# Row transforms of a spectral layer as pairs of 64-column products, and the last loads moved to ScalarE's queue

## The chip, the cores and the metric

One core of a Trainium2 chip runs the whole program. The metric is device time in microseconds (us) of one execution. Everything is computed in 32-bit floats (F32), except for some operands of the attention that the kernel splits in two parts.

## What is computed

The input is an image of 48 x 48 tokens (T = 2304) with C = 768 channels. A transformer block comes first: layer norm, attention over all tokens with relative positions, a projection, and an MLP with a hidden width of 3072. A spectral layer follows, and the change lies at its two ends. Cut to what matters:

```python
# layer 0
x = shortcut + attention(layernorm(x)) @ proj_w + proj_b
x = x + gelu(layernorm(x) @ mlp_w1 + mlp_b1) @ mlp_w2 + mlp_b2
# layer 1 (H = W = 48, 8 blocks of 96 channels)
bias = x
xf = rfft2(x, axes=(1, 2), norm='ortho').reshape(B, 48, 25, 8, 96)
o1r = relu(xr @ w1[0] - xi @ w1[1] + b1[0]);  o1i = relu(xi @ w1[0] + xr @ w1[1] + b1[1])
o2r = softshrink(o1r @ w2[0] - o1i @ w2[1] + b2[0], 0.01);  o2i = ...
y = irfft2(o2r + 1j * o2i, s=(48, 48), axes=(1, 2), norm='ortho')
return y + bias
```

## The kernel before, in words

**Stages.** The program runs in one order: queries, keys and values, attention, projection, the MLP, the spectral layer. The block's result stays on chip as `x1` (128 tokens x 18 tiles x 768 channels, in the tile `main`). The channels of the spectral layer are worked in two halves of CH = 384.

**The order of the work.** TensorE's order in the MLP and in the spectral layer is written out by hand (`tc.manual_schedule(engines={PE})`, lines 1109 and 1306). The other engines and the queues are ordered by the framework's scheduler, which may bring a load forward in SyncE's queue. In the whole kernel every transfer is issued on SyncE's queue (named SP, or SPq where its issues are listed). Each engine works through its own queue in order, and an issue of a transfer waits for its data, for its buffer, and for an earlier transfer whose semaphore it uses again; there are eight such semaphores, used in turn.

**Forward row transform** (`rows_forward`, line 1069). The MLP runs in three blocks p of 768 tokens, and after each one the rows of that block are transformed along the width. A row has 48 tokens, and its 25 frequencies have a real and an imaginary part: 50 numbers. A group g of 384 tokens is 8 rows, three tiles of 128 tokens. The result of a group is cut into four parts `zp` of two rows (100 partitions x 384 channels), each of which takes one or two products with a constant of 128 x 100, `rows_dft[:, b]`: six products per group and channel half. Each part is copied out of its PSUM bank (tags o0 to o3, one bank each, which the MLP's second layer shares) into a tile `zt` (eight buffers), by ScalarE for p = 0 and 1 and by VectorE and ScalarE in turn for p = 2, and stored to `z1` in HBM, where a row takes 50 lines of 384 channels.

**Middle of the spectral layer** (class `Unit`, line 1180). Fourteen units (two channel halves, seven sets of up to four frequencies; the last set has one) pass through four steps. `load` fetches `zi` from z1 (`load_frequencies`, line 937; the first two units' loads are issued within `rows_forward` at p = 2). `columns` transforms along the height (`fp`), `first` and `second` are the two layers (`lp`, `l1`, `mp`), and `back` transforms back along the height (`yp`, one PSUM bank) and stores `y` to `z2` in HBM. In round r of the main loop unit r is at `columns`, r - 1 at `first`, r - 2 at `second` and r - 3 at `back`, with four steps i in a round.

**Inverse row transform** (`rows_back`, line 1281). For a group of 384 tokens and one channel half, one load brings `zo` (100 partitions x 4 x 384) from z2, which needs that all frequencies of that half are in z2. Then three output tiles `rps` of 128 tokens take two products each (100 x 128 constants `irows`), VectorE adds x1 into `yt` (four buffers), and SyncE stores it to the output. `rps` has the two banks of tag f, which `fp` also uses, and zo has three buffers. The generators of the first half are advanced by one step in each step i of the rounds r > 11: one step in four is a load, three are pieces (a piece is one output tile). So 12 pieces stand in TensorE's order ahead of the last `yp`, and 24 after it: six of the first half and 18 of the second.

Of the kernel before, what the change touches and what calls it, by code (L numbers as in the profile page):

```python
# [9 lines left out]
F32 = mybir.dt.float32  # L10
# [34 lines left out]
def block_then_afno(  # L45
# [47 lines left out]

    z1 = [dram.tile([HW * 2 * KW, CH], F32, name=f"z1_{k}") for k in range(2)]
    z2 = [dram.tile([HW * 2 * KW, CH], F32, name=f"z2_{k}") for k in range(2)]
# [841 lines left out]
    def load_frequencies(half, k0):  # L937

        rows = z1[half].rearrange("(r k) c -> r k c", k=KW)
        tiles = []  # L940
        for k in range(k0, min(k0 + 4, KW), 2):
            n = min(2, KW - k)
            zi = turn.tile([P, C], F32, name="zi", tag="turn")
            zi = zi[: 2 * HW].rearrange("p (k c) -> p k c", c=CH)
            nc.sync.dma_start(out=zi[:, :n], in_=rows[:, k : k + n, :])
            tiles.append(zi)
        return tiles

    with ExitStack() as mlp:
        bias = mlp.enter_context(tc.tile_pool(name="mlp_const", bufs=1))  # L950
        b2 = bias.tile([P, C], F32, name="b2")
        nc.sync.dma_start(out=b2, in_=mlp_b2[0, :].partition_broadcast(P))
        rows_dft = bias.tile([P, 6, 2 * 2 * KW], F32, name="rows_dft")
        nc.sync.dma_start(out=rows_dft, in_=c_rows)
# [114 lines left out]
        def rows_forward(p):  # L1069

            for k in range(2):
                for g in (2 * p, 2 * p + 1):
                    for a, parts in enumerate(((0,), (1, 2), (3, 4), (5,))):
                        zp = psum.tile([2 * 2 * KW, CH], F32, name="zp", tag=f"o{a}")
                        for b in parts:
                            nc.tensor.matmul(  # L1076
                                zp, rows_dft[:, b, :], x1[:, 3 * g + b // 2, ts(k, CH)],
                                start=(b == parts[0]), stop=(b == parts[-1]),
                            )
                        zt = turn.tile([2 * 2 * KW, CH], F32, name="zt", bufs=8)  # L1080
                        if p < 2:
                            nc.scalar.copy(zt, zp)
                        else:
                            balanced_copy(a, zt, zp)
                        nc.sync.dma_start(out=z1[k][ts(4 * g + a, 4 * KW), :], in_=zt)
                if (p, k) == (2, 0):
                    first_loads.extend(load_frequencies(0, k0) for k0 in (0, 4))
# [39 lines left out]
    with ExitStack() as sp:  # L1127
# [153 lines left out]
        def rows_back(half, g):  # L1281

            zo = zin.tile([4 * KW, 4, CH], F32, name="zo", bufs=3)
            nc.sync.dma_start(
                out=zo, in_=z2[half][ts(g, 16 * KW), :].rearrange("(a p) c -> p a c", a=4)
            )
            yield
            for i in range(3):
                yt = mid.tile([P, CH], F32, name="yt", bufs=4)
                rp = psum.tile([P, CH], F32, name="rps", tag="f")  # L1290
                for e in range(2):
                    nc.tensor.matmul(  # L1292
                        rp, irows[:, 2 * i + e, :], zo[:, i + e, :], start=(e == 0), stop=(e == 1)
                    )
                nc.vector.tensor_tensor(yt, rp, x1[:, 3 * g + i, ts(half, CH)], ALU.add)
                nc.sync.dma_start(out=out[ts(3 * g + i, P), ts(half, CH)], in_=yt)
                yield
# [3 lines left out]

        def pieces(gens):
            for gen in gens:
                yield from gen

        with tc.manual_schedule(engines={mybir.EngineType.PE}):
            first_half = pieces(ends[0])
            for r in range(len(units) + 3):
                if r < len(units):
                    units[r].load()  # L1310
                for i in range(4):
                    for stage, lag in (("back", 3), ("second", 2), ("first", 1), ("columns", 0)):
                        if 0 <= r - lag < len(units):
                            getattr(units[r - lag], stage)(i)
                    if r > len(units) // 2 + 4:
                        next(first_half, None)
            for _ in first_half:
                pass
            for _ in pieces(ends[1]):
                pass  # L1320


def _constants():
# [18 lines left out]

    fr = np.stack([cos[:, :KW], -sin[:, :KW]], 1).reshape(n, 2 * KW)

# [5 lines left out]

    fwd = np.zeros((8 * n, 8 * 2 * KW))
    inv = np.zeros((8 * 2 * KW, 8 * n))
    for r in range(8):
        fwd[r * n : (r + 1) * n, r * 2 * KW : (r + 1) * 2 * KW] = fr
        inv[r * 2 * KW : (r + 1) * 2 * KW, r * n : (r + 1) * n] = ir
    rows = np.zeros((P, 6, 4 * KW))
    irows = np.zeros((4 * KW, 6, P))
    for b in range(6):
        t, a = b // 2, (b + 1) // 2
        rows[:, b] = fwd[t * P : (t + 1) * P, a * 4 * KW : (a + 1) * 4 * KW]  # L1360
        irows[:, b] = inv[a * 4 * KW : (a + 1) * 4 * KW, t * P : (t + 1) * P]
# [87 lines left out]
```

## Time and profile before

| | us |
|---|---|
| median of three runs | 2929.87 |
| the three runs | 2922.76, 2929.87, 2933.12 |
| the profiled execution | 2924.9 |
| its span, first to last instruction | 2922.9 |
| zp stage at p = 0, first zp product to first product behind the stage | 1965.66 to 1981.47 |
| zp stage at p = 1 | 2313.21 to 2328.69 |
| zp stage at p = 2 | 2655.91 to 2671.5 |
| middle of the spectral layer, first fp to end of the last yp | 2672.1 to 2881.15 |
| tail: end of the last yp to end of span | 2881.15 to 2922.9 |

All times of places are counted from the span's start. A product in F32 leaves two records in the trace, each with its own load of weights, so a stage of 24 products shows 48. The ends of records on TensorE are modelled and overlap the next one's start, so durations are best read from start to start. "Idle before" names what ended an engine's wait.

### The profile page before, as it was taken

Reading aid. Unit: us, or ns where it says so; the run is one execution under the profiler, and the core shown is the slowest. Engines: PE = TensorE matmul, PEld = TensorE weight load, DVE = VectorE, ACT = ScalarE, POOL = GpSimd, SP = SyncE. Lnnn points to the kernel's source line nnn. Section 1 sums busy time; section 2 is a strip of 40 time slices with the busy share of each in tenths; the row PEclk is TensorE's granted clock in tenths of the full one; section 3 lists DMA queues with packets and bytes.
Section 4 is the critical chain, followed back from the end, with each engine's and each line's share of the span. In section 5 each row is a group of like instructions: output and inputs, shape, how many; then the busy total and the mean of one; then the engine's idle time right before and its main releaser. Section 6 shows DMA issues by size and latency. Waiting matters only on the chain. (4 is left out here: it accounts for less than half of the span.)

```text
span 2922.9 us, 40961 instructions
## 1 busy us (share of the span) xinstructions
PE 2864.6 (98%) x15659; PEld 1724.2 (59%) x15659; DVE 1791.0 (61%) x2606; ACT 936.3 (32%) x1514; POOL 609.8 (21%) x564
## 2 busy tenths in 40 slices
PE   7999999999999999999999999999999999999998
PEld 4555665555555555555555555555555555556885
DVE  5243237777777777777733666674666566665564
ACT  1011126656666565665500211122011211102331
POOL 2302110000000000000043322343332323222441
PEclk9999999999999999999999999999999999999999
DMA  3423276173462716435252111212121212113235
GB/s 127 148 88 118 92 162 123 30 135 64 82 128 41 144 34 101 109 59 87 56 177 76 43 56 53 65 64 65 57 65 54 77 54 65 54 57 99 79 93 179
DMA packets 202818, 253.03 MB, mean 87 GB/s; under 512 B 21618, under 2 KB 180978, under 8 KB 201078
## 3 DMA queue, kind: packets, MB, share of 16 engines
q1 hardware_dynamic: 202614, 250.32, 33.5%
q8 instruction: 126, 2.06, 0.3%
q14 instruction: 78, 0.64, 0.1%
HBM read 136.40 MB, written 50.14 MB: 64 GB/s over the span
## 5 line engine op out<-in xcount | busy, mean ns | idle before, releaser
L635 DVE TENSOR_TENSOR acc<-acc,main 128x768 f32<-128x768 f32 x576 | 551.9, 958 | 206.4 <-ACT main L569 149.9
L569 ACT ACTIVATE main<-sp 128x768 f32<-128x768 f32 x648 | 520.8, 812 | 138.9 <-PE sp L565 132.2
L565 PE MATMUL sp<-terms,select 64*128 64x384 f32 x1296 | 413.3, 630 | 0.0
L1051 DVE TENSOR_TENSOR main<-o,main 128x384 f32<-128x384 f32 x540 | 299.4, 557 | 40.3 <-PE o L1049 2.1
L989 PE MATMUL h<-shared,w 128*128 128x384 f32 x864 | 296.7, 486 | 0.8 <-issue 0.8
L559 PE MATMUL sp<-shared 64*128 64x384 f32 x1296 | 268.0, 490 | 2.5 <-DVE o L457 2.2
L559 PE MATMUL sp<-qT,kT 64*128 64x384 f32 x1296 | 266.7, 487 | 0.2
L612 POOL TENSOR_TENSOR inverse<-inverse,rden 128x384 f32<-128x384 f32 x36 | 46.3, 1287 | 1010.7 <-DVE rden L609 918.1
L446 PE MATMUL m<-main 128*128 128x384 f32 x756 | 247.0, 488 | 6.4 <-DVE rstd L121 3.0
L989 PEld LDWEIGHTS h<-shared,w 128*128 128x128 f32 x864 | 164.4, 190 | 116.1 <-issue 2.3
L989 PE MATMUL h<-shared,w1s 128*128 128x384 f32 x648 | 226.6, 486 | 0.0
L582 PE MATMUL op<-main,shared 128*64 128x384 f32 x1296 | 221.2, 488 | 0.0
L582 PE MATMUL op<-main,v 128*64 128x384 f32 x1296 | 219.9, 488 | 0.0
L995 ACT ACTIVATE hT<-c,vec 128x384 f32<-128x384 f32 x108 | 66.4, 615 | 466.2 <-DVE c L1001 466.1
L446 PEld LDWEIGHTS m<-main 128*128 128x128 f32 x756 | 142.6, 190 | 108.3 <-issue 8.7
L1001 DVE TENSOR_TENSOR c<-h,u 128x384 f32<-128x384 f32 x108 | 60.2, 557 | 212.3 <-PE h L989 212.3
L1049 PE MATMUL o<-w,hT 128*128 128x384 f32 x432 | 175.0, 487 | 3.0 <-DVE mv L118 2.0
L1049 PE MATMUL o<-w2s,hs 128*128 128x384 f32 x432 | 174.8, 487 | 3.1 <-DVE hs L155 3.1
L565 PEld LDWEIGHTS sp<-terms,select 64*128 64x128 f32 x1296 | 125.8, 187 | 83.9 <-issue 0.5
L989 PEld LDWEIGHTS h<-shared,w1s 128*128 128x128 f32 x648 | 123.1, 190 | 85.9
L154 POOL TENSOR_TENSOR w1s<-w 128x384 f32<-128x384 f32 x36 | 36.4, 1010 | 610.9 <-PE o L1049 289.4
L559 PEld LDWEIGHTS sp<-shared 64*128 64x128 f32 x1296 | 117.9, 187 | 61.3 <-issue 23.1
(158 smaller groups left out, 3896.8 us busy)
## 6 DMA issues: line engine op xcount, KB each, us to landing
w<-in_mlp_w_dram SPq DMA_DIRECT2D x72, 768.0 KB
terms<-col_parts SPq DMA_DIRECT2D x432, 72.0 KB
terms<-row_hi SPq DMA_DIRECT2D x216, 72.0 KB
terms<-row_lo SPq DMA_DIRECT2D x216, 72.0 KB
main<-in_qkv_w_dram SPq DMA_DIRECT2D x36, 384.0 KB
z<-zt SPq DMA_DIRECT2D x48, 150.0 KB
zo<-z SPq DMA_DIRECT2D x12, 600.0 KB
x<-in_x_dram SPq DMA_DIRECT2D x18, 384.0 KB
```

Of the source, the lines that this page charges most:

```text
L446: nc.tensor.matmul(bank, a[:, c, :], b[:, c, :], start=(first and c == 0), stop=(c == 2), skip_group_check=not first,)
L559: nc.tensor.matmul(sp[:, j, :G], kT[at, ts(kt, P)], qT[at, ts(c, G)], start=True, stop=False,)
L565: nc.tensor.matmul(sp[:, j, :G], select[at, a % 2], ready[pr, c][at, a // 2, b], start=False, stop=True,)
L569: nc.scalar.activation(p, sp[:, :, :G], AF.Exp, scale=HD**-0.5)
L582: nc.tensor.matmul(op[ts(j, 64)], v[:, kt0 + i, ts(j, 64)], ps[i][:, j, :], start=(kt0 + i == 0), stop=(kt0 + i == NT - 1),)
L612: nc.gpsimd.tensor_tensor(inverse, inverse, rden, ALU.add)
L635: nc.vector.tensor_tensor(acc, made[0] if kt == 1 else acc, p, ALU.add)
L989: nc.tensor.matmul(bank[i], a[:, c, :], b[:, c, :], start=(start and c == 0), stop=(c == 2), skip_group_check=not start,)
L995: nc.scalar.activation(h[:, i, ts(k, G)], src, AF.Gelu, bias=col(V_B1 + 2 * n + i))
L1001: nc.vector.tensor_tensor(t, src, other, ALU.add)
L1049: nc.tensor.matmul(bank[k], a, b, start=start, stop=True, skip_group_check=not start)
L1051: nc.vector.tensor_tensor(dst, bank[k], dst, ALU.add)
```

## The change

It has four parts.

1. Forward rows: the result of one row, padded from 50 to 64 lines, is one product with a constant of 128 x 64 (`rows_dft[:, i, r]`: tile i of three, row r of eight). Each output bank holds two rows, one in each half of the 128 partitions, and so in each half of TensorE's columns. Ten products per group replace six; they stand in TensorE's order as five pairs whose two products write different halves. z1 now has 64 lines a row. zt becomes one tile of four parts with two buffers.
2. Inverse rows: an output tile's two halves of 64 tokens are products of their own with 100 x 64 constants. Eight products per group, as four pairs of different halves, replace six. The three output tiles use the tags f, m and l, two banks each.
3. Buffers and queues: two of every five zo tiles take a buffer of zt's, so that there are five; the loads of the second channel half are issued on ScalarE's queue instead of SyncE's.
4. Order: three loads of the first half are started together in round 12, and three pieces a round are done in rounds 13 to 16, in their steps 0 to 2. Four loads of the second half are started ahead of what is left of the first half. In the changed kernel's instruction order nine pieces stand ahead of the last yp, and 27 after it.

```diff
@@ -91,7 +91,7 @@
 
     dram = ctx.enter_context(tc.tile_pool(name="scratch", bufs=1, space=DRAM))
 
-    z1 = [dram.tile([HW * 2 * KW, CH], F32, name=f"z1_{k}") for k in range(2)]
+    z1 = [dram.tile([HW * 64, CH], F32, name=f"z1_{k}") for k in range(2)]
     z2 = [dram.tile([HW * 2 * KW, CH], F32, name=f"z2_{k}") for k in range(2)]
     q_d = [dram.tile([P, T], F32, name=f"q_d{i}") for i in range(NC)]
     k_d = [dram.tile([P, T], F32, name=f"k_d{i}") for i in range(NC)]
@@ -936,7 +936,7 @@
 
     def load_frequencies(half, k0):
 
-        rows = z1[half].rearrange("(r k) c -> r k c", k=KW)
+        rows = z1[half].rearrange("(r k) c -> r k c", k=32)
         tiles = []
         for k in range(k0, min(k0 + 4, KW), 2):
             n = min(2, KW - k)
@@ -950,7 +950,7 @@
         bias = mlp.enter_context(tc.tile_pool(name="mlp_const", bufs=1))
         b2 = bias.tile([P, C], F32, name="b2")
         nc.sync.dma_start(out=b2, in_=mlp_b2[0, :].partition_broadcast(P))
-        rows_dft = bias.tile([P, 6, 2 * 2 * KW], F32, name="rows_dft")
+        rows_dft = bias.tile([P, 3, 8, 64], F32, name="rows_dft")
         nc.sync.dma_start(out=rows_dft, in_=c_rows)
 
         psum = mlp.enter_context(tc.tile_pool(name="ps_mlp", bufs=1, space=PSUM))
@@ -1070,19 +1070,28 @@
 
             for k in range(2):
                 for g in (2 * p, 2 * p + 1):
-                    for a, parts in enumerate(((0,), (1, 2), (3, 4), (5,))):
-                        zp = psum.tile([2 * 2 * KW, CH], F32, name="zp", tag=f"o{a}")
-                        for b in parts:
+
+
+                    zp = []
+                    for pair in (((0, 0), (0, 1)), ((0, 2), (1, 3)), ((1, 2), (1, 5)),
+                                 ((1, 4), (2, 5)), ((2, 6), (2, 7))):
+                        for i, r in pair:
+                            if r // 2 == len(zp):
+                                zp.append(psum.tile([P, CH], F32, name="zp", tag=f"o{len(zp)}"))
                             nc.tensor.matmul(
-                                zp, rows_dft[:, b, :], x1[:, 3 * g + b // 2, ts(k, CH)],
-                                start=(b == parts[0]), stop=(b == parts[-1]),
+                                zp[r // 2][ts(r % 2, 64)], rows_dft[:, i, r],
+                                x1[:, 3 * g + i, ts(k, CH)],
+                                start=((i, r) not in ((1, 2), (2, 5))),
+                                stop=((i, r) not in ((0, 2), (1, 5))), skip_group_check=True,
                             )
-                        zt = turn.tile([2 * 2 * KW, CH], F32, name="zt", bufs=8)
+                    zt4 = turn.tile([P, 4, CH], F32, name="zt", bufs=2)
+                    for a in range(4):
+                        zt = zt4[:, a]
                         if p < 2:
-                            nc.scalar.copy(zt, zp)
+                            nc.scalar.copy(zt, zp[a])
                         else:
-                            balanced_copy(a, zt, zp)
-                        nc.sync.dma_start(out=z1[k][ts(4 * g + a, 4 * KW), :], in_=zt)
+                            balanced_copy(a, zt, zp[a])
+                        nc.sync.dma_start(out=z1[k][ts(4 * g + a, P), :], in_=zt)
                 if (p, k) == (2, 0):
                     first_loads.extend(load_frequencies(0, k0) for k0 in (0, 4))
 
@@ -1280,31 +1289,54 @@
 
         def rows_back(half, g):
 
-            zo = zin.tile([4 * KW, 4, CH], F32, name="zo", bufs=3)
-            nc.sync.dma_start(
+            if (T // G * half + g) % 5 in (1, 3):
+                zo = turn.tile([P, 4, CH], F32, name="zo2", tag="zt", bufs=2)[: 4 * KW]
+            else:
+                zo = zin.tile([4 * KW, 4, CH], F32, name="zo", bufs=3)
+            (nc.scalar if half else nc.sync).dma_start(
                 out=zo, in_=z2[half][ts(g, 16 * KW), :].rearrange("(a p) c -> p a c", a=4)
             )
             yield
-            for i in range(3):
+
+
+            rp = []
+            for a, pair in enumerate(
+                (((0, 0), (0, 1)), ((1, 0), (0, 1)), ((2, 0), (1, 1)), ((2, 0), (2, 1)))
+            ):
+                if a < 3:
+                    rp.append(psum.tile([P, CH], F32, name="rps", tag="fml"[a]))
+                for i, j in pair:
+                    shared_half = (i, j) in ((0, 1), (2, 0))
+                    nc.tensor.matmul(
+                        rp[i][ts(j, 64)], irows[:, a + i, ts(j, 64)], zo[:, a, :],
+                        start=(not shared_half or a % 2 == 0),
+                        stop=(not shared_half or a % 2 == 1), skip_group_check=shared_half,
+                    )
+                if a == 0:
+                    continue
+                i = a - 1
                 yt = mid.tile([P, CH], F32, name="yt", bufs=4)
-                rp = psum.tile([P, CH], F32, name="rps", tag="f")
-                for e in range(2):
-                    nc.tensor.matmul(
-                        rp, irows[:, 2 * i + e, :], zo[:, i + e, :], start=(e == 0), stop=(e == 1)
-                    )
-                nc.vector.tensor_tensor(yt, rp, x1[:, 3 * g + i, ts(half, CH)], ALU.add)
+                nc.vector.tensor_tensor(yt, rp[i], x1[:, 3 * g + i, ts(half, CH)], ALU.add)
                 nc.sync.dma_start(out=out[ts(3 * g + i, P), ts(half, CH)], in_=yt)
                 yield
 
         units = [Unit(half, k0) for half in range(2) for k0 in range(0, KW, 4)]
         ends = [[rows_back(half, g) for g in range(T // G)] for half in range(2)]
 
-        def pieces(gens):
-            for gen in gens:
-                yield from gen
+        def in_turn(gens, ahead):
+
+            for gen in gens[:ahead]:
+                next(gen)
+            yield
+            for g, gen in enumerate(gens):
+                for _ in range(3):
+                    next(gen)
+                    yield
+                for gen in gens[g + ahead : g + ahead + 1]:
+                    next(gen)
 
         with tc.manual_schedule(engines={mybir.EngineType.PE}):
-            first_half = pieces(ends[0])
+            first_half, second_half = in_turn(ends[0], 3), in_turn(ends[1], 4)
             for r in range(len(units) + 3):
                 if r < len(units):
                     units[r].load()
@@ -1312,11 +1344,13 @@
                     for stage, lag in (("back", 3), ("second", 2), ("first", 1), ("columns", 0)):
                         if 0 <= r - lag < len(units):
                             getattr(units[r - lag], stage)(i)
-                    if r > len(units) // 2 + 4:
-                        next(first_half, None)
+
+                    if (r, i) == (len(units) - 2, 3) or (r > len(units) - 2 and i < 3):
+                        next(first_half)
+            next(second_half)
             for _ in first_half:
                 pass
-            for _ in pieces(ends[1]):
+            for _ in second_half:
                 pass
 
 
@@ -1340,7 +1374,8 @@
             select[32 + 16 * part + w, :, :, w] = 1.0
 
 
-    fr = np.stack([cos[:, :KW], -sin[:, :KW]], 1).reshape(n, 2 * KW)
+    fr = np.zeros((n, 2, 32))
+    fr[:, 0, :KW], fr[:, 1, :KW] = cos[:, :KW], -sin[:, :KW]
 
     twice = np.full((KW, 1), 2.0)
     twice[[0, KW - 1]] = 1.0
@@ -1348,16 +1383,16 @@
     si[[0, KW - 1]] = 0.0
     ir = np.concatenate([cos[:KW] * twice, -si], 0)
 
-    fwd = np.zeros((8 * n, 8 * 2 * KW))
+
+    fwd = np.zeros((8 * n, 8, 64))
     inv = np.zeros((8 * 2 * KW, 8 * n))
     for r in range(8):
-        fwd[r * n : (r + 1) * n, r * 2 * KW : (r + 1) * 2 * KW] = fr
+        fwd[r * n : (r + 1) * n, r] = fr.reshape(n, 64)
         inv[r * 2 * KW : (r + 1) * 2 * KW, r * n : (r + 1) * n] = ir
-    rows = np.zeros((P, 6, 4 * KW))
+    rows = fwd.reshape(3, P, 8, 64).transpose(1, 0, 2, 3)
     irows = np.zeros((4 * KW, 6, P))
     for b in range(6):
         t, a = b // 2, (b + 1) // 2
-        rows[:, b] = fwd[t * P : (t + 1) * P, a * 4 * KW : (a + 1) * 4 * KW]
         irows[:, b] = inv[a * 4 * KW : (a + 1) * 4 * KW, t * P : (t + 1) * P]
```

## Prediction

> **What bounds the kernel now.** I read the page's head, then the chain of waits in order of time, then the timelines of TensorE and of the DMA queue around the lines that change, then the transfer rates of two stretches.
>
> ```profile
> PE 2864.6 (98%) x15659; PEld 1724.2 (59%) x15659; DVE 1791.0 (61%) x2606; ACT 936.3 (32%) x1514; POOL 609.8 (21%) x564
> ```
>
> TensorE is busy 98% of the span, so a product saved is time saved wherever its successor is ready. The chain says where that is so:
>
> ```profile
> 2313.37 15.48 PE zp L1076 x48
> 2328.85 17.41 PE h L989 x54
> ...
> 2656.07 15.49 PE zp L1076 x48
> 2881.31 6.17 PE rps L1292 x20
> 2887.49 6.80 DMA zo<-z
> 2898.29 7.30 DMA zo<-z
> 2909.60 5.73 DMA zo<-z
> 2915.47 4.12 PE rps L1292 x12
> ```
>
> Columns: start, length, engine, records. The three zp stages stand in the chain with TensorE alone. A product leaves two records, 15.48/48 = 0.3225 us each, so a product is 0.645 us. From 2881 us on loads of zo alternate with products: the tail is a matter of transfers.
>
> ```profile
> 999.86 4.04 PE L582 MATMUL op<-main,v 128*64 128x384 f32 x24
> 1003.83 0.92 PE L559 MATMUL sp<-qT,kT 64*128 64x384 f32 x4
> ...
> 2313.21 15.64 PE L1076 MATMUL zp<-main,rows_dft 128*100 128x384 f32 x48
> 2328.69 2.10 PE L989 MATMUL h<-shared,w 128*128 128x384 f32 x6
> ...
> 2890.02 4.11 PE L1292 MATMUL rps<-zo,shared 100*128 100x384 f32 x12 [0.96 <-DMA zo<-z]
> ```
>
> L582 already does what the change does: weights of 64 columns, alternate outputs in the two partition halves. 24 records (12 products) took 1003.83 - 999.86 = 3.97 us, 6 x 0.645 = 3.87 and 0.10 for the change of shape. A pair costs one product.
>
> ```profile
> 2883.88 0.32 SPq L1284 DMA_DIRECT2D zo<-z  x1
> 2884.52 2.91 SPq L1296 DMA_DIRECT2D out_dram<-yt  x3
> 2887.49 0.41 SPq L1284 DMA_DIRECT2D zo<-z  x1
> 2888.39 5.40 SPq L1296 DMA_DIRECT2D out_dram<-yt  x4
> 2893.88 0.32 SPq L1284 DMA_DIRECT2D zo<-z  x1
> ```
>
> In SyncE's queue each load stands behind stores that wait for VectorE; little more than one load is in flight.
>
> ```profile
> 2785.50:2788.00 2.50, 2.50 (x29) 2.50 (x28) 1.07 (x3) 1.49 (x4) 1.19 (x2) 1.00 0.66 229
> 2888.00:2915.00 27.00, 21.59 (x64) 11.29 (x62) 9.03 (x17) 0.00 (x0) 0.00 (x0) 1.00 0.76 245
> ```
>
> The last two columns are the DMA share and GB/s. The first stretch has zo loads alone: 0.66 of 16 engines is ten and a half, at 229 GB/s. The second is the tail: 0.76 only, yet TensorE idles 5.4 of 27 us.
>
> **What the Trainium skill says.** "TensorEngine Tiling (Array Packing)", Tiling Modes, Key Properties: tiles load weights and multiply in parallel, and a change of tiling mode drains the array. L582 agrees with both (pair 0.645 us, change about 0.10). "DMA: Bandwidth & Descriptors", Why a DMA increments its semaphore by 16 and not by 1: a transfer over 100 partitions runs on ten engines, over 128 or 96 on sixteen. The 0.66 agrees. The same page, Issuing engines are not separate DMA queues: ScalarE's transfers run on the same sixteen engines, so the new queue saves waiting in order, not bandwidth. All transfers here are on one queue, so no trace shows it. Its Latency and other measured facts: row pitches in HBM cost at 2 MiB and more, not at 512 KiB; z1's rows go from 38,400 to 49,152 bytes. No run here shows a pitch; I take zero.
>
> **The change, part by part.**
>
> *Forward rows (L1069).* A group of 384 tokens and 384 channels had 6 products, and gets 10 in 5 pairs: one slot of 0.645 us less, times 12 groups = 7.74 us. VectorE and GpSimd, which feed and follow, are done in time: at p = 0 the last add to the first channel half ends at 1967.4 (its reader, the second group, starts at 1965.66 + 3.23 = 1968.9), the differences for the next block (L172) end at 1969.5. Against it: two changes of shape in each of three stages, 0.6. At p = 0 ScalarE's copies stand behind rstd, which waits for VectorE until 1972.05: 0.3. At p = 2 the first columns need zi, which moves up by only the two groups' 1.29 us: 0.3, ends 0 and 1.3. Net 6.5.
> The copies grow from 100 to 128 partitions: nothing (zt 479 ns at 100, ot 479 ns at 128). Stores grow from 150 to 192 KB but go from ten engines to sixteen. The zt tile now holds four quarters in two buffers: the third group's first copy waits for all four stores of the first. A group lasts 3.23 us, then a pair of 0.645; copy 0.48 and landing 1.95 (z<-y issued 2881.93, its reader 2883.88) fit. Zero; if not, the group's other copies queue behind it, TensorE waits for their banks of zp, and it costs some 0.5 per stage. The table load grows from 300 to 768 KB at 1624.93; its first reader is at 1965 and the next load 12 us behind: zero.
>
> *Inverse rows ahead of the tail (L1281, L1311).* The last yp ends at 2881.15. Before it stand 12 pieces (an output tile of two products) x 1.29 = 15.48 us. After, pieces start a round later, three a round: 9 of 0.86 us on average (4 pairs for three) = 7.74. Saved 7.74. Against it: each of 9 pieces enters and leaves the pair shape, 18 x 0.10 = 1.8. The piece that stood ahead of a round's first mp covered GpSimd's o; uncovered it waits 0.4 (at 2794.99 and 2781.65), three times, and yp has one bank, which a shorter piece covers less: 0.5. Net 4.2, ends 2 and 7.7. Five zo loads instead of three go ahead of zi loads, ten engines for 5 x 2.6 = 13 us; the last zi, issued 2800.74, is read at 2845.16. Hidden.
>
> *The tail.* Now 2922.9 - 2881.15 = 41.75 us, for 24 pieces. After: 27 pieces (gens 3 to 5 of the first half, then the second half), 27 x 0.86 = 23.2 us of TensorE, then yt 0.56 and a store of 2.7: at least 26.7. The loads start 2.75 us after the last yp (2883.88 - 2881.15), as now, for they need all of z2; nine pieces (7.74 us) cover that and most of the first landing. Loads go to ScalarE's queue, behind the last y copy, with nothing behind them; SyncE loses six waits. So the transfers decide: on each of the ten engines 6 x 614 KB/10 = 369 KB of loads and 27 x 197 KB/16 = 332 KB of stores. At 229/10 = 22.9 KB/us, or 24 with the queue never empty, all but the last stores (some 610 KB) take 25.4 us. From 3.7 us (issue and first byte) the last load lands at 29; three pieces, yt and store end at 35. Waits of yt's four buffers fall inside this. I take 34.5: 7.25 saved. From below, TensorE alone with a stall of 1: 28. From above: at today's 245 GB/s, 9.0 MB take 36.7, with start and end 42, nothing saved.
>
> Sum: 6.5 + 4.2 + 7.25 = 18. The profiled run took 2924.9 (span 2922.9 and 2.0 around it): 2907. The median of the three runs, 2929.87, lies 5.0 above; on that scale 2912.
>
> **Rivals.**
> - *Transfers keep their rate.* For: 0.76 in the tail is what ten full engines and six at a third give. Against: engines idle between loads now (6.0 to 7.3 us from issue to landing where 614 KB alone take 2.6). Then only 10.7 comes: 2919.
> - *TensorE paces the tail.* For: four loads ahead, and stores that spread. Tail 28, and fewer stalls in the rounds: 6.5 + 6 + 13.7 = 26: 2904. Against: ten engines with 700 KB each.
> - *The pairs don't overlap* (slower). In zp and rps the two products of a pair read different tiles at times, and rps has 100 rows. One after the other: 4 more products in 12 groups, 31.0 us; 9 pieces at 1.72 are as long as 12 at 1.29; tail 27 x 1.72 + 2.8 = 49.2, 7.5 more: about 2968. It decides from a pair of some 1.45 products (0.94 us). Against: L582 reads two tiles too and shows 0.66 with its drain.
>
> **How the numbers follow.** Forecast (tail 31 to 38): 0.56, time 2907 to 2917. Rates kept: 0.16. TensorE-paced: 0.18. No overlap: 0.05. A wait not seen here that eats most of it, no change: 0.05. The likeliest is 2912. Low end: the second rival with a run as low as the lowest shown (7 below the median): 2897. High end: the first rival and 2 us of scatter: 2921. Beyond lie the last two cases and edges. A measurement tells 0.3%, 8.8 us, from no change: faster means below 2921. Forecast, TensorE-paced and three quarters of the first rival: 0.86. Same 0.08; slower 0.06.
>
> **What would show it.** zp stages of 40 x 0.3225 = 12.9 us, not 15.5. The last yp some 10.7 us earlier. Six output tiles of rps in 5.2 us of TensorE, not 7.7. In the tail a DMA share near 0.8 to 0.9, more GB/s than 245, several zo in flight, waits of rps for zo shorter. If the zp stages stay at 15 us or more, the pairs failed; if the tail is 40 or more, the transfers took the gain; if TensorE never waits for zo, my bound on ten engines was wrong.

## The result, and the profile after

The changed kernel takes 2915.44 us (median of seven runs, 2911.76 to 2920.12), the kernel before 2929.17 on the same chip (seven runs, 2922.76 to 2933.12): 13.7 us less, ratio 0.9959 with a 95% interval of 0.9946 to 0.9971. The profiled execution took 2914.89, its span is 2912.8, 10.1 less than before.

Totals scatter by 5 us and more, and so do profiles: the first zp product at p = 0, ahead of all changed work but the larger load of the table, came at 1965.66 before and at 1968.21 after. So the stages are compared by their own lengths, from start to start. At p = 2 the zp stage is counted up to the first fp, which starts at 2672.12 before. Over fourteen profiles the lengths of unchanged stages agree far better than the totals: in the twelve that have the new zp stage, it takes 13.05 or 13.06 us at p = 1 in eleven, and 13.17 in one. Tails of the same code agree less well: 36.86, 37.15 and 37.23 us in three profiles of the new one, 41.75 and 42.47 in two of the old. So a difference of less than some 0.7 us between two tails is not read as an effect.

| us | before | after | shorter | predicted |
|---|---|---|---|---|
| three zp stages | 15.81 + 15.48 + 16.21 | 13.68 + 13.05 + 14.14 | 6.6 | 6.5 |
| middle, first fp to end of the last yp | 209.03 | 207.42 | 1.6 | 4.2 |
| tail, end of the last yp to end of span | 41.75 | 37.23 | 4.5 | 7.25 |
| sum | | | 12.8 | 18 |

The head of the page after: TensorE has 144 records more and is busy 18.6 us less.

```profile
PE 2846.0 (98%) x15803; PEld 1702.9 (58%) x15803; DVE 1791.4 (61%) x2606; ACT 934.8 (32%) x1514; POOL 614.1 (21%) x564
```

TensorE's timeline around the zp stage at p = 1 (start, length, line, shapes, records). Eighty records of four groups follow one another without a gap, and the next product starts 13.05 us after the first: 40 records in sequence of 0.326 us. Two products of a pair take the time of one.

```profile
2313.73 13.12 PE L1081 MATMUL zp<-main,rows_dft 128*64 128x384 f32 x80
2326.78 2.20 PE L989 MATMUL h<-shared,w 128*128 128x384 f32 x6
```

The same view at the end of the rounds. A piece in a round is one pair (x4) or, for the first of a group, two (x8); the last yp waits 0.70 us for a copy out of its only bank; then 12 pairs run in 7.96 us.

```profile
2863.99 1.52 PE L1261 MATMUL mp<-shared,o 96*96 96x96 f32 x16
...
2866.50 1.35 PE L1261 MATMUL mp<-shared,o 96*96 96x96 f32 x14
2868.19 0.41 PE L1261 MATMUL mp<-shared,o 96*96 96x96 f32 x2 [0.34 <-POOL o L1247]
2868.53 1.51 PE L1310 MATMUL rps<-zo,shared 100*64 100x384 f32 x8
2869.97 0.89 PE L1280 MATMUL yp<-zz,shared 96*96 96x384 f32 x2
...
2874.78 0.86 PE L1280 MATMUL yp<-zz,shared 96*96 96x384 f32 x2 [0.70 <-ACT y L75]
2875.57 7.96 PE L1310 MATMUL rps<-zo,shared 100*64 100x384 f32 x48
2884.78 2.80 PE L1310 MATMUL rps<-zo,shared 100*64 100x384 f32 x16 [1.25 <-DMA zo<-z]
```

The windows of the middle and the tail (span of the window, busy us of PE, PEld, DVE, ACT, POOL, granted clock, DMA share, GB/s), first the tail before, then both after. In the tail TensorE works 26.4 of 37.2 us; the rate of the transfers rose from 215 to 254 GB/s, and the clock fell from 0.99 to 0.94.

```profile
2881.15:2922.90 41.75, 32.55 (x97) 17.54 (x95) 14.05 (x26) 0.00 (x0) 0.00 (x0) 0.99 0.66 215
```

```profile
2668.15:2875.57 207.42, 200.27 (x1685) 173.04 (x1685) 120.70 (x272) 77.87 (x216) 87.91 (x106) 1.00 0.33 99
2875.57:2912.80 37.23, 26.40 (x145) 11.53 (x144) 15.20 (x28) 0.00 (x0) 0.00 (x0) 0.94 0.72 254
```

Who waited in the tail (total, times, longest), before and after. VectorE's yt waited for stores for 3.5 us; now it is 17.2, and TensorE's waits for zo are no shorter (5.2 before, 5.9 after).

```profile
PE rps L1292 <- DMA zo<-z: 5.2, 5, 1.6
DVE yt L1295 <- DMA out_dram<-yt: 3.5, 2, 2.0
```

```profile
DVE yt L1319 <- DMA out_dram<-yt: 17.2, 15, 2.2
...
PEld rps L1310 <- DVE yt L1319: 7.2, 8, 2.9
PE rps L1310 <- DMA zo<-z: 5.9, 4, 2.3
```

The chain of the tail (start, length, what) goes from store to store and ends with the last load, which lands 30.0 us after the last yp.

```profile
2878.36 4.63 DMA out_dram<-yt
...
2883.69 5.59 DMA out_dram<-yt
...
2889.99 5.96 DMA out_dram<-yt
...
2895.97 0.04 ACTq L1296
...
2896.04 9.48 DMA zo<-z
2905.53 0.14 issue
2905.66 2.81 PE rps L1310 x16
```

Four loads were to be ahead, but the issues in ScalarE's queue come 2.7, 3.3, 7.5, 13.5, 16.2 and 20.5 us after the last yp. The program's own waits tell one reason: every transfer of SyncE and ScalarE takes the next of eight semaphores in turn and waits until that one's last transfer has landed. The second and the fourth load have the same one, called DMAHW4 here:

```
zo_42230<-z2_1_71 100x4x384 [waits DMAHW4_49]
zo2_42232<-z2_1_71 100x4x384 [waits DMAHW0_49,PE_49]
zo_42234<-z2_1_71 100x4x384 [waits DMAHW4_49,PE_49]
```

### The profile page after: what moved, and what is told of

It is laid out like the page before. It is cut to its first block, busy times and chain, and to the rows that moved or that the text cites. A ratio compares the mean times of both kernels' runs of the same rounds, so it can differ in the third digit from the quotient of the medians.

```text
span 2912.8 us, 41244 instructions
## 1 busy us (share of the span) xinstructions
PE 2846.0 (98%) x15803; PEld 1702.9 (58%) x15803; DVE 1791.4 (61%) x2606; ACT 934.8 (32%) x1514; POOL 614.1 (21%) x564
```

## The experiments

The theory of the prediction for the tail is called the ten engines: loads over 100 partitions run on ten of the sixteen DMA engines, and these set the pace. The profile gives only the mean share of all sixteen, so that it is these ten can't be seen in it directly. The rivals are the four tiles of yt (VectorE's 17 us of waits), the semaphores above, ScalarE's queue, and TensorE's own time. All runs gave these stage lengths in their profiles (us), and these ratios to the kernel before, each against runs on its own chip:

| run | zp stages | middle | tail | tail's share, GB/s | ratio (95%) |
|---|---|---|---|---|---|
| before | 47.50 | 209.03 | 41.75 | 0.66, 215 | |
| after | 40.87 | 207.42 | 37.23 | 0.72, 254 | 0.9959 (0.9946 to 0.9971) |
| fwd_only | 40.58 | 209.36 | 42.47 | 0.64, 211 | 0.9973 (0.9962 to 0.9984) |
| inv_only | 47.34 | 207.28 | 36.86 | 0.73, 256 | 0.9973 (0.9963 to 0.9982) |
| wide | 40.87 | 208.59 | 38.34 | 0.69, 247 | 0.9969 (0.9957 to 0.9980) |
| on_sync | 40.38 | 207.41 | 39.76 | 0.69, 238 | 0.9962 (0.9950 to 0.9975) |
| zo96 | 40.45 | 207.44 | 39.93 | 0.77, 236 | 0.9957 (0.9943 to 0.9971) |
| yt10 | 40.41 | 207.40 | 37.68 | 0.71, 251 | 0.9949 (0.9934 to 0.9964) |
| zo96_yt10 | 40.16 | 211.28 | 39.53 | 0.77, 239 | 0.9964 (0.9952 to 0.9977) |
| p123 | 41.26 | 205.01 | 37.15 | 0.74, 259 | 0.9942 (0.9929 to 0.9956) |
| pool_loads | 40.81 | 207.41 | 40.49 | 0.78, 233 | 0.9964 (0.9952 to 0.9977) |
| st2 | 40.87 | 207.42 | 37.67 | 0.71, 251 | 0.9948 (0.9933 to 0.9962) |
| zo128 | 40.58 | 207.41 | 35.58 | 0.83, 289 | 0.9944 (0.9929 to 0.9959) |
| joined | 40.83 | 204.97 | 35.34 | 0.83, 296 | 0.9933 (0.9917 to 0.9949) |

Most intervals overlap, so the ratios alone can't rank single edits; the stage that an edit touches can.

### The two halves of the change apart

fwd_only is the kernel before with the changed kernel's `rows_forward`, z1 and constant; inv_only is the changed kernel with these taken back, all but the zt tile of four parts:

```diff
-                    for pair in (((0, 0), (0, 1)), ((0, 2), (1, 3)), ...
+                    zt4 = turn.tile([P, 4, CH], F32, name="zt", bufs=2)
+                    for a, parts in enumerate(((0,), (1, 2), (3, 4), (5,))):
```

> Only the forward row transform is changed; the inverse part is that of the kernel before. In the profile of the changed kernel the three zp stages are 2.13, 2.43 and 2.07 us shorter (13.68, 13.05 and 14.14 against 15.81, 15.48 and 16.21), 6.6 in all. If the stages are worth what they show: 6.6 us faster than before, ratio 0.9977. Rival, that what follows takes it back (larger stores, rows of z1 further apart, copies in four-quarter tiles): 0 to 3 us, ratio 0.999 to 1.000.

> Only the inverse part is changed (pairs in rps, order, loads ahead, ScalarE's queue); the forward products are those of the kernel before, but copied into the changed kernel's tile of four quarters. If the parts add up: the profiles give 1.6 us from the middle and 4.5 from the tail, 6.1, and the medians 13.7 - 6.6 = 7.1; so 6 to 7 us faster than before, ratio 0.9976 to 0.9980. If the two parts only work together (each waits for the other): under 3 us, ratio above 0.999.

fwd_only took 2922.31 us against 2928.72, inv_only 2918.54: 6.4 and 10.2 less. By stages they are 6.9 shorter in zp, and 1.75 + 4.89 = 6.6 shorter in middle and tail; each leaves the stages of the other within 0.8 us of what they were before. By stages the parts add up to 13.6, where both together gave 12.8; the medians give 16.6 against 13.7, apart by less than their intervals. So neither part needs the other, and the total of fwd_only shows nothing behind the forward rows that takes their gain back.

### wide: the new order with the old products

```diff
+            for i in range(3):
+                rp = psum.tile([P, CH], F32, name="rps", tag="fml"[i])
+                for e in range(2):
+                    nc.tensor.matmul(
+                        rp, irows[:, 2 * i + e, :], zo[:, i + e, :], start=(e == 0), stop=(e == 1)
+                    )
```

> The changed kernel with the old products of the inverse (two of 128 columns for each output tile, 1.29 us a tile instead of 0.86), in the new order, with the new loads and queue. Theory of the ten engines (transfers pace the tail): 27 tiles take 34.8 us of TensorE, with store at the end 38, against 37.2 now; the nine tiles in the rounds leave and enter no other shape, 3 x 3.9 = 11.7 instead of 10.5. Together about 2 us slower than the changed kernel: 11 to 12 us faster than before, ratio 0.996. Rival, that TensorE's time is what made the tail shorter: 27 x 0.43 = 11.6 us in the tail come back, at least half of them, and the gain against before is 2 to 8 us, ratio 0.9973 or above.

TensorE's timeline of this run shows the whole tail as one stretch: 27 tiles of 1.29 us, and not one wait for zo.

```profile
2876.16 35.00 PE L1305 MATMUL rps<-zo,shared 100*128 100x384 f32 x108
```

The pairs save 27 x 0.43 = 11.6 us of that, and the tail is 1.1 us shorter with them (38.34 to 37.23), the middle 1.2. In the changed kernel's tail TensorE is busy for 26.4 us and idle for 10.8; here it is busy for 35.0 and idle for 3.3. So most of what the pairs save comes back as waits, and some of it as records at a lower clock (0.94, here 1.00). What shortens the tail from 41.75 to 38.3 is the order with its banks, buffers and loads ahead, which were not taken apart further; below that TensorE's time no longer decides. The total (2917.17 us, ratio 0.9969) lies between the two expectations, and its interval holds both.

### on_sync: the second half's loads back on SyncE's queue

```diff
-            (nc.scalar if half else nc.sync).dma_start(
+            nc.sync.dma_start(
```

> The changed kernel with the second half's zo loads issued by SyncE among the stores, as before, still four ahead. Theory of the ten engines: the same bytes on the same engines, and two to three loads stay in flight, so the tail stays within 1.5 us of 37.2 and the time within 1.5 us of the changed kernel, ratio to before 0.995 to 0.9965. Rival, the queue: each load again stands behind stores that wait for VectorE, the tail goes back to 40 to 42 us, and the gain against before falls to 9 to 10 us, ratio 0.9968.

The tail is 39.76 us, 2.5 longer: outside what the ten engines allowed, and near the rival's number, but not by its mechanism. The first four loads did not stand behind waiting stores; they were issued within 5.6 us, ahead of most stores, and the stores waited behind them. (The fifth and the sixth did stand behind four stores each, at 12.7 and 22.4 us, but TensorE shows no wait for them.) One wait of yt for a store took 9.4 us, and TensorE stood still behind it:

```profile
2883.53 0.87 PE L1310 MATMUL rps<-zo,shared 100*64 100x384 f32 x4 [0.79 <-DMA zo<-z]
2890.81 15.25 PE L1310 MATMUL rps<-zo,shared 100*64 100x384 f32 x76 [6.41 <-DVE yt L1319]
```

Behind this gap TensorE ran to the end of its work without a wait, but at half clock until 26.1 us of the tail: 76 records took 15.25 us, where 48 at full clock take 7.96 and 76 so some 12.6. Part of this stretch is on the chain that ended last, 36 records in 8.83 us. So the 2.5 us are about what the half clock took, and the order in the queue cost them by way of the gap. That is one profile; the median (2915.09) is that of the changed kernel within scatter, so a gain of the second queue is not shown in the time.

### yt10: ten yt tiles in the second half

```diff
+                if half and (3 * g + i) % 5 in (1, 3, 4):
+                    yt = turn.tile([P, C], F32, name="yt2", tag="turn")[:, :CH]
+                else:
+                    yt = mid.tile([P, CH], F32, name="yt", bufs=4)
```

> The changed kernel with ten yt tiles instead of four in the second half, six of them in the tiles that held zi. Theory of the store buffers: VectorE's waits for stores (17 us in the tail) mostly vanish, TensorE no longer waits for banks, tail 31 to 34 instead of 37.2, ratio to before about 0.994. Theory of the ten engines: stores only queue deeper on the same engines; TensorE's waits go over to zo; within 1.5 us of the changed kernel, ratio 0.9954 to 0.9962.

Tail 37.68, where the theory of the yt tiles wanted 31 to 34. VectorE's waits for stores went from 17.2 to 6.3 us, and TensorE's for zo from 5.9 to 7.0; the wait only changed its name.

```profile
PE rps L1310 <- DMA zo<-z: 7.0, 4, 3.3
```

There is one thing against this reading. The last 48 records are at the end of the chain, and they took 10.91 us, where 48 at full clock take 7.96:

```profile
2896.98 10.91 PE L1310 MATMUL rps<-zo,shared 100*64 100x384 f32 x48 [3.27 <-DMA zo<-z]
```

So the half clock took up to 2.9 us of this tail. But the loads came no sooner: this wait ended 23.4 us after the last yp (22.0 in the changed kernel), and the last packet of ScalarE's queue 30.6 us after it (29.3). With a last group, its addition and its store behind that (2.8 + 0.56 + 2.7 us), the tail would have been some 36.7 us at full clock too, an estimate from these numbers. The theory of the yt tiles falls.

### zo96 and zo96_yt10: the loads as two transfers

```diff
+            rows = z2[half][ts(g, 16 * KW), :].rearrange("(a p) c -> p a c", a=4)
+            for p in (slice(0, 96), slice(96, 4 * KW)):
+                (nc.scalar if half else nc.sync).dma_start(out=zo[p], in_=rows[p])
```

> The changed kernel with each zo load cut in two transfers, partitions 0 to 95 and 96 to 99. Theory of the ten engines: 96 partitions spread over sixteen, so an engine carries 6 x 38 = 230 KB of loads instead of 369, and with 332 KB of stores 562 KB instead of 701; at 22.9 KB/us that is 6 us less, of which TensorE's 23.2 us of pairs and their waits leave 3 to 6: tail 31 to 34 instead of 37.2, 17 to 19 us faster than before, ratio 0.9937 to 0.9945. Theory of the store buffers (VectorE waits for a store to free one of yt's four tiles, 17 us in the tail): within 1 us of the changed kernel, or slower by the twelve extra issues.

> Both edits: zo loads as 96 and 4 partitions, and ten yt tiles in the second half. Theory of the ten engines: as with the split loads alone, and up to 2 us more, since sixteen engines at 22.9 KB/us need 24.6 us for 9.0 MB and TensorE's 23.2 plus the ends then decide: tail 29 to 32, ratio to before 0.993. Theory of the store buffers: as with ten tiles alone, 0.994. If neither matters, 0.996.

Both miss: tails of 39.93 and 39.53 us. The share rose (0.77), the rate fell (236 GB/s). A load's packet took 0.096 us on average instead of 0.071, the twelve issues needed 29.3 us after the last yp instead of 20.5, and stretches of 393 GB/s alternate with stretches of 81. Which of the two, slower packets or the issues of twice as many transfers, holds it back was not separated, and in zo96 some 1.8 us at half clock stand at the end of the chain (32 records in 7.07 us); the edit changes all of these, and so is no test of the ten engines.

### zo128: the loads over 128 partitions in one transfer

```diff
+            src = z2[half][ts(g, 16 * KW), :].rearrange("(a p) c -> p a c", a=4)
+            if g < T // G - 1:
+                src = bass.AP(tensor=src.tensor, offset=src.offset, ap=[[CH, P], *src.ap[1:]])
+            (nc.scalar if half else nc.sync).dma_start(out=zo[: src.shape[0]], in_=src)
```

> The changed kernel with each zo load but the last of a half taken over 128 partitions in one transfer (28 more rows of the next quarter, which no product reads): as many transfers as before, 786 KB on sixteen engines, 49 KB an engine, instead of 614 KB on ten, 61. Theory of the ten engines: an engine carries 5 x 49 + 61 + 332 = 638 KB instead of 701, 2.8 us less at 22.9 KB/us: tail 34 to 35. Theory of the semaphores: loads are issued as late as before and land some 0.5 us sooner each where one is alone: tail 36 to 37.5.

Here the number of transfers stays; five of the six loads read 28 rows more, which no product uses. The Trainium skill, "DMA: Bandwidth & Descriptors", section Why a DMA increments its semaphore by 16 and not by 1, gives the rule: the largest number up to 16 that divides the slowest dimension, ten for 100 and sixteen for 128. The trace agrees, as far as a mean share can. Windows of 16 us while loads run, first of the changed kernel, then of zo128, both from 5.4 us of the tail on:

```profile
2881.00:2897.00 16.00, 10.93 (x64) 4.65 (x60) 5.01 (x9) 0.00 (x0) 0.00 (x0) 1.00 0.79 285
```

```profile
2876.00:2892.00 16.00, 13.16 (x72) 4.63 (x68) 5.10 (x10) 0.00 (x0) 0.00 (x0) 1.00 1.06 386
```

From 0.79 of the engines and 285 GB/s to all of them and 386. The tail is 35.58 us, though it moves 0.9 MB more; 1.65 us shorter than in the changed kernel, more than tails of the same code differ by. It lies between the two expectations, 34 to 35 for the ten engines and 36 to 37.5 for the semaphores, so the length alone does not choose between them; the share, the rate and the waits do. TensorE's waits for zo drop from 5.9 to 0.9 us, and yt's waits for stores (14.4 us, as against 17.2) are then the longest:

```profile
DVE yt L1321 <- DMA out_dram<-yt: 14.4, 14, 2.6
```

### st2 and pool_loads: the semaphores

```diff
+                if half:
+                    if j % 2 == 0:
+                        y2[0] = turn.tile([P, C], F32, name="yt2", tag="turn")
+                    yt = y2[0][:, ts(j % 2, CH)]
...
+                elif j % 2:
+                    nc.sync.dma_start(
+                        out=out[ts(j // 2, 2 * P), ts(half, CH)].rearrange("(t p) c -> p t c", p=P),
+                        in_=y2[0].rearrange("p (t c) -> p t c", t=2),
+                    )
```

```diff
-            (nc.scalar if half else nc.sync).dma_start(
+            (nc.gpsimd if half else nc.sync).dma_start(
```

> The changed kernel with the second half's output tiles stored two by two: 9 stores of 384 KB instead of 18 of 192, from tiles that held zi (12 output tiles instead of 4). Theory of the semaphores: 15 transfers instead of 24 take turns on eight; the fourth load waits for an early store instead of the second load, the fifth and sixth for transfers further back; tail 34 to 36 us instead of 37.2. Theory of the ten engines: same bytes on the same engines, tail 36.5 to 38. (Ten single tiles changed the tail by 0.5 us, so the tiles themselves are not it.)

> The changed kernel with the second half's zo loads issued from GpSimd's queue instead of ScalarE's. New theory, the semaphores: the program gives every transfer issued by SyncE or ScalarE one of eight semaphores in turn, and an issue waits until the last transfer on its semaphore has landed, so that loads 3 to 6 were issued 7.5, 13.5, 16.2 and 20.5 us after the last yp and not ahead; GpSimd's transfers have semaphores of their own in this program. Then loads 1 to 4 are issued within some 6 us (load 4 waits for a buffer until 5.3), TensorE hardly waits for zo after the first, and the tail is 33 to 35 us instead of 37.2 if ten engines at 22.9 KB/us then pace it, 30 to 32 if they don't. Rival, the ten engines alone: the queue of the issue changes nothing, 37 to 38, or longer by GpSimd's work for a transfer.

With stores by twos the fourth, fifth and sixth load are issued at 11.0, 12.1 and 18.7 us instead of 13.5, 16.2 and 20.5, and the tail is 37.67: issuing earlier gains nothing. From GpSimd's queue four loads are issued within 6.1 us and the fifth at 8.3, and the tail is 40.49, outside both expectations. This one is not clean. The share is 1.02, so the loads no longer leave engines idle, yet the rate (281 GB/s) is no higher than the changed kernel has at 0.79; and the clock is 0.68 in this window.

```profile
2883.00:2899.00 16.00, 13.44 (x52) 5.23 (x52) 3.35 (x6) 0.00 (x0) 0.84 (x1) 0.68 1.02 281
```

So the semaphores are real and delay the loads, but by st2 what they delay would only queue at the engines.

### p123: the pieces one step later in their round

```diff
-                    if (r, i) == (len(units) - 2, 3) or (r > len(units) - 2 and i < 3):
+                    if (r, i) == (len(units) - 2, 3) or (r > len(units) - 2 and i > 0):
```

> The changed kernel with the pieces of a round behind steps 1, 2 and 3 of the round instead of 0, 1 and 2, so that one stands ahead of the next round's first mp. Theory: the three waits of mp for GpSimd's (and once ScalarE's) o in the rounds with pieces, which cost 0.6, 1.0 and 0.6 us by the distance to the next lp, are covered: the last yp comes about 2 us earlier after the first fp (205.4 instead of 207.4). The time is 1 to 2 us less than the changed kernel's if the tail moves with it. Rival: the wait only moves to the copies of y (yp has one bank) or to the start of the tail, since z2's last rows are stored later behind the last piece: no change.

Middle 205.01 us (expected 205.4), tail 37.15, time 2912.72. In rounds with pieces no mp waits for o any more, nor does the last yp for its bank; the only wait left there is that of the round ahead of the first piece:

```profile
2837.43 0.41 PE L1261 MATMUL mp<-shared,o 96*96 96x96 f32 x2 [0.40 <-POOL o L1247]
```

A wait of 0.40 us costs more than it shows. In the changed kernel mp takes 2.00 us with it (2835.24 to 2837.24, start to start), and 1.36 without (2857.11 to 2858.47):

```profile
2835.24 1.35 PE L1261 MATMUL mp<-shared,o 96*96 96x96 f32 x14
2836.99 0.41 PE L1261 MATMUL mp<-shared,o 96*96 96x96 f32 x2 [0.40 <-POOL o L1247]
2837.24 0.49 PE L1230 MATMUL lp<-xf,shared 96*96 96x192 f32 x2
...
2857.11 1.52 PE L1261 MATMUL mp<-shared,o 96*96 96x96 f32 x16
2858.47 0.29 PE L1230 MATMUL lp<-xf,shared 96*96 96x48 f32 x2
```

### joined: zo128, st2 and p123 together

> The changed kernel with the three edits that helped or may help where another limit is gone: zo over 128 partitions in one transfer, the second half's output tiles stored two by two, the pieces of a round behind steps 1 to 3. Theory (ten engines paced the tail, and with sixteen the stores hold VectorE back, 14.4 us of waits for four yt tiles): middle 205.0 as with the moved pieces; loads of 4.55 MB and stores of 5.3 MB at 390 GB/s take 25 us from 4.2 us on, and the last products and stores some 4: tail 32 to 34.5 us instead of 37.2; with 6.6 from the forward rows 18 to 20 us faster than before, ratio 0.993 to 0.994. Rival, that paired stores take back what wider loads give (fewer, longer transfers, and an output tile waits for its partner): tail 35.5 to 37, ratio 0.9945.

2907.84 us against 2929.27, ratio 0.9933 (0.9917 to 0.9949): the lowest time of all, 21.4 us below the kernel before. The middle is as expected (204.97), the tail of 35.34 is not: above 32 to 34.5 and just below the rival's range. Stores by twos add nothing to the wide loads that would stand clear of scatter (35.34 against 35.58). Its interval and that of the changed kernel (0.9946 to 0.9971) meet at the edges, and the two were not run side by side; by stages it is 40.83 + 204.97 + 35.34 = 281.1 us against 40.87 + 207.42 + 37.23 = 285.5. Why the tail stays above 35 us with sixteen engines is open. The profile names the sixth load, still over 100 partitions, issued 14.3 us after the last yp and landed 12.5 us later, and then a last group at half the clock (16 records in 4.35 us, 2.8 elsewhere), which is 1.5 us on the chain:

```profile
2884.69 12.50 DMA zo<-z
2897.18 0.14 issue
2897.32 4.35 PE rps L1314 x16
```

## Why the prediction was right, and which terms were off

The predicted time, 2912, lies 3.4 us below the median, and 2915.44 is within the forecast's 2907 to 2917, near its slow end. The direction and the bound of the tail held. By stages 12.8 us came of 18: one of the three terms was met, the other two were too high, and no error was made good by another. That the total was met in spite of this owes something to the width of the range.

- **A pair costs one product: right.** 13.05 us for 40 records in sequence is 0.326 each (0.3225 predicted), and 12 pairs of rps in 7.96 us are 0.66 each, so six output tiles 5.3 us (5.2 predicted). No pair is near the 0.94 from which the slow rival would decide.
- **Forward rows, 6.5: right,** 6.6 (6.9 in fwd_only). Longer copies, larger stores and z1's wider rows took nothing back that shows in the total.
- **Middle, 4.2: too high, 1.6,** which is below even its lower end of 2. All three costs were seen and undersized. A piece cost 1.30 us before and, in rounds of 1.61 + 0.96 + 0.96, on average 1.16 after (1.57 + 0.92 + 0.92 in the short round), so twelve pieces of 15.7 became nine of 10.5. Of that 2.7 us are above the pairs' 7.74, where 1.8 were put down: entering and leaving the shape costs 0.30 a piece, not 0.20. GpSimd's o cost 0.6 + 1.0 + 0.6 = 2.2, not 1.2, since a wait was priced by its idle time alone. The yp bank cost 0.86 (2873.92, where the yp would have stood by the distances of the rounds, to 2874.78), not 0.5. 5.2 - 2.2 - 0.86 leaves 2.1; 1.6 was measured, and the 0.5 between them is not explained. p123 gives 2.4 of these 3.1 us of waits back.
- **Tail, 34.5: too low, 37.2, within its 31 to 38; its bound right.** A share of 0.79 of sixteen fits ten full engines and the rest in part; it gave 285 GB/s, 22.5 GB/s for each engine's worth of share (22.9 to 24 taken). The last load landed at 30.0 us, where 29 was worked out; but it was issued only at 20.5, so loads that follow one another from the start, as the sum had them, are not how it came about. Behind it 7.3 us were needed, not 6: four pairs, and VectorE with tiles of two groups still to add because yt had waited for stores. Of the difference of 2.7 to the value taken, 1.0 is the load, 1.3 the end, and 0.5 the step from a worked-out 35 to 34.5. The sum "at least 26.7" comes to 26.5, which nothing rests on. Two signs named did not show: a share of 0.8 to 0.9 was not reached over the tail (0.72), only nearly in its middle (0.79), and the waits of rps for zo grew from 5.2 to 5.9 us. Wide, st2 and yt10 moved TensorE's time, the issues and yt's waits without moving the tail by more than 1.1 us, and in zo128 the edit that lets the loads fill all engines shortened it by 1.65. So transfers on the engines decide; that exactly ten were full is inferred.
- **"Four loads ahead" was taken at its word: wrong, without harm.** Waits of ScalarE's queue were not looked at beyond the first load. st2 says that they cost nothing as long as these engines are full.
- **Waits of yt's four buffers "fall inside this": right** for the time: of 17.2 us of waits yt10 removes 10.9, for nothing.
- **What the prediction did not have: the half clock.** It took TensorE at full clock throughout (27 x 0.86 = 23.2 us in the tail); the last section shows what the waits did to it.
- **Rivals.** "Transfers keep their rate" was half true: 0.79 and 285 GB/s over 16 us of loads, against 0.76 and 245 before. "TensorE paces the tail" is refuted by wide, where 11.6 us more of TensorE's work lengthen the tail by 1.1.

## What to carry to other kernels

When two engines and the transfers take turns in a tail, as here, removing one's work may move the waits and little else: work out the bytes on the DMA engines that a transfer really uses, and see whether the partition count lets it use all of them, before counting saved products. Price a step that is put between other steps by the distance from start to start of its neighbours with and without it, not by its own length or the idle time shown; both were too low here. And where totals scatter by more than the effect, compare the lengths of the stages that an edit touches.

## What had not been expected of the hardware

Short gaps in TensorE's work can be followed by half its clock. In the changed kernel, after a wait of 2.25 us, 32 records took 7.23 us, where 5.3 is usual:

```profile
2897.57 7.23 PE L1310 MATMUL rps<-zo,shared 100*64 100x384 f32 x32 [2.25 <-DMA zo<-z]
```

The clock record is at 0.50 for 3.4 us, from 22.2 to 25.6 us of the tail; in windows of 2 us:

```profile
2896.00:2898.00 2.00, 0.43 (x2) 0.23 (x4) 0.56 (x1) 0.00 (x0) 0.00 (x0) 0.93 0.75 283
2898.00:2900.00 2.00, 2.00 (x8) 0.90 (x6) 1.00 (x2) 0.00 (x0) 0.00 (x0) 0.50 0.76 280
2900.00:2902.00 2.00, 2.00 (x10) 0.80 (x7) 0.78 (x3) 0.00 (x0) 0.00 (x0) 0.72 0.85 316
```

The Trainium skill, "TensorE: Matmul & The Clock Gate", Part 1, says that the clock is either full or half and is set by a free-running window of about 3.4 us; the values and the 3.4 agree. It asks for an idle window of that length, and here less was enough: 2.25 us in this run, and in zo96_yt10 three gaps of 0.58, 0.89 and 0.56 us within 5 us, behind which the middle ran 6.8 us at half clock and became 3.9 us longer than in the other runs, gaps included. Where the limit lies, no run here shows. At the same place of the middle the changed kernel had gaps of 1.02 and 0.56 us and ran on at full clock. The tail before had six gaps of up to 1.63 us between stretches of 4.1, and its clock was 0.99:

```profile
2905.73 4.11 PE L1292 MATMUL rps<-zo,shared 100*128 100x384 f32 x12 [1.63 <-DMA zo<-z]
```

In wide, where TensorE never waits, the tail ran at 1.00; in every other tail with the new order it was 0.82 to 0.94. What that costs in the changed kernel's tail is about 1.9 us of TensorE's time; since a load landed later, it needn't be on the path. In on_sync, yt10, zo96 and joined it is, as said there. No run took it away alone.
